# The first layer's transposed activations: by TensorE, or by a round trip through DRAM and 32x32 squares on VectorE

## The chip, the cores and the metric

The kernel runs on one core of one Trainium2 chip. The metric is the device time of one execution in microseconds, as the median of several runs; before the change it is 1163.4 us, the median of three runs that lie between 1161.4 and 1163.57 us. Everything is in float32. The engines are named as the profile names them: PE is TensorE (PEld is its weight load), DVE is VectorE, ACT is ScalarE, POOL is GpSimd, SP is SyncE, which here only issues DMAs.

## The reference

Four sequences (B = 4) of N = 1024 tokens with D = 256 channels pass two layers. Only the first is touched by the change:

```python
xn = layernorm(x)                         # no weights
x = x + attention(xn) + ffn(xn)           # first layer
#   attention: q = xn Wq, k = xn Wk, v = xn Wv; causal softmax(q k^T / 16) v;
#              layernorm(out + v) * gamma + beta; then Wfc, bfc
#   ffn:       relu(xn W1 + b1) W2 + b2, 1024 hidden units
xn = layernorm(x)
x = x + gated_linear_attention(xn) + top2_of_8_experts(xn)   # second layer
```

The second layer has a gated attention in groups of 64 tokens, and eight experts with low-rank additions, of which each token takes two.

## The kernel before, in words

**Tiles.** 128 tokens lie on the 128 partitions. The first layer works in 16 units of 256 tokens (two token tiles); unit `u` is part `p = u % 4` of sequence `b = u // 4`. Scores of a unit reach back over all units of its sequence, so a unit with p = 3 has about four times the score work of one with p = 0.

**A unit's steps**, as functions of `block_kernel`:

- `first(u)`: mean and variance of 256 tokens, and `xn` (tokens on partitions), on DVE with a little ACT. `xn` has seven buffers, so it runs well ahead.
- `first_turn(u)` (line 423): four PE transposes of 128x128 (line 427) put `xn` with its channels on partitions into a PSUM bank; ACT copies the bank to `xnT` in SBUF (line 429; six buffers). A matmul needs `xnT` wherever the contraction runs over channels.
- `queries(u)` (line 439): eight PE records on `xnT`, copied by ACT to `qT` (line 446).
- `scores(u, qT)` (line 449): `sc` in PSUM from `qT` and the `xnT` of all units of the sequence so far; DVE adds the mask (line 461) and takes the maximum (line 463), ACT the exponential (line 466), DVE the reciprocal and the scaling (lines 468, 469).
- `turns` (line 487): PE transposes of the attention weights; ACT copies those of the first token tile, DVE those of the second (line 495), to `attT`.
- `hidden` (line 473): the first matmul of the feed-forward part, `relu` on ACT (line 483).
- `weighted` (line 497): `pz` from `xn` and `attT`; DVE adds `xnT` and writes `zT` (line 507).
- `finish` (line 512): second feed-forward matmul `po` (line 520) and the value product `pv` (line 524), added to x by DVE (lines 526, 533).
- `norms`, `norms_turn`, `logits` (lines 537 to 587): norms for the second layer, four PE transposes (line 566), ACT copy to `xlT` (line 571) and, for b > 0, a store of `xlT` to DRAM (line 573).
- `merge` (line 379): loads a piece of an expert's weights (`wt`, `lt`), multiplies its low-rank pair on PE (lines 397 to 400), adds it on DVE (line 403) and stores the sum to DRAM (lines 404, 406). `fold_second` (line 349) does a small preparation once; its tile `bb` shares the buffers of `zT`.

**Order.** The loop at line 662 runs over the units. In iteration u stand: `turns(u)` and the first half of `hidden(u)`, `first_turn(u + 2)`, `queries(u + 1)`, `norms_turn(u - 1)`, `weighted(u)`, `logits(u - 1)`, `scores(u + 1)`, the rest of `hidden(u)`, `first(u + 3)`, `finish(u)`, `norms(u)`. The tile framework puts each engine's instructions into one fixed order when the program is built, by its own estimate of when each can start; on the chip every engine, and every engine's DMA queue, takes them strictly in that order and stands still at one that has to wait. PSUM banks of the first layer are four in rotation for nearly everything (`p_mm`, through `bank`), and two double banks for scores and `merge` (`p_sc`).

**After the first layer** come the second layer's attention for sequence 0, the table of experts, 36 blocks of 256 gathered tokens for the experts (`blocks`), and the attention of sequences 1 to 3 with the gathering and adding of the experts' results. The experts' blocks already use the way that the change brings to the first layer: `rows(i)` (line 792) reads 256 rows of 256 floats from DRAM with four DMAs of 64 KB that place runs of 32 floats so that each 32x32 square lies on its target partitions, and `turn` (line 810) transposes the squares with one DVE instruction (line 812).

Of the kernel before, what the change touches and what calls it, by code (L numbers as in the profile page):

```python
# [9 lines left out]
F32 = mybir.dt.float32  # L10
# [7 lines left out]
P = 128  # L18
B, N, D = 4, 1024, 256
NT = N // P  # L20
DC = D // P
# [41 lines left out]
def block_kernel(ctx: ExitStack, tc: tile.TileContext, x, wq, wk, wv, wfc, w1, w2, wqk, wvl, wg,  # L63
                 wo, wr, ew, el, eb2, cols, rows, rope, posb, out):
    nc = tc.nc
    pers = ctx.enter_context(tc.tile_pool(name="pers", bufs=1))
    small = ctx.enter_context(tc.tile_pool(name="small", bufs=3))
    NP = NT // 2
# [27 lines left out]
    def col(name, i=0):  # L96
        n = COLS[name][0] + i
        return colt[:, n : n + 1]

    def row(name):  # L100
        n, w = ROWS[name]
        return rowt[:, n - RE : n - RE + w]
# [56 lines left out]
    dram = ctx.enter_context(tc.tile_pool(name="dram", bufs=1, space=DRAM))  # L159
    wm13 = dram.tile([E, P, W13], F32, name="wm13")  # L160
    wm2 = dram.tile([E, P, W2B], F32, name="wm2")
    xg = dram.tile([E * RS, D], F32, name="xg")
    yg = dram.tile([NBLK * TB, D], F32, name="yg")
    xld = [dram.tile([P, DC, N], F32, name=f"xld{b}") for b in range(B)]

    def stats(src, mv, t, tag="st"):
        st = small.tile([P, 6], F32, tag=tag, name="st")
        w = nc.vector.bn_stats(st, src)  # L168
        nc.vector.bn_aggr(mv[:, t, :], st)  # L169
        return w.ins  # L170
# [21 lines left out]
    def rstd_of(var, tag, n=NT):  # L192
        rstd = small.tile([P, n], F32, tag=tag, name="rstd")
        rsqrt(rstd, var)
        return rstd

    def normalise(dst, src, mv, rstd, t):
        nc.vector.tensor_scalar(dst, src, mv[:, t, 0:1], rstd[:, t : t + 1], ALU.subtract, ALU.mult)
# [25 lines left out]
    with ExitStack() as l0:  # L224
# [7 lines left out]
        def bank(shape, name):  # L232
            return p_mm.tile(shape, F32, tag="mm", name=name)

        act = l0.enter_context(tc.tile_pool(name="l0a", bufs=2))
# [110 lines left out]
            return raw  # L346

        def fold_second(raw):
            bb = act.tile([P, DC, P], F32, tag="zT", name="bb")
            for c in range(DC):  # L350
                nc.gpsimd.tensor_copy(bb[:, c, :], col("ln1_b", c).to_broadcast([P, P]))
            for w, name, n in ((raw, "bqk", QK), (wvl_s, "bv", H1)):
                pm = bank([P, n], "pm")
                for c in range(DC):
                    nc.tensor.matmul(pm, bb[:, c, :], w[:, c, :], start=(c == 0), stop=(c == DC - 1))
                nc.vector.tensor_tensor(row(name), pm, row(name), ALU.add)
            pm = bank([P, HC], "pm")
            for m in range(HC):
                for c in range(DC):
                    nc.tensor.matmul(pm[:, m : m + 1], wg_s[:, c, ts(m, P)], col("ln1_b", c),  # L360
                                     start=(c == 0), stop=(c == DC - 1))
            n = COLS["bg"][0]
            nc.vector.tensor_tensor(bg_s, pm, colt[:, n : n + HC], ALU.add)
            with tc.issue_after(finish.sq):
                for c in range(DC):
                    nc.scalar.mul(wqr_s[:, c, 0:QK], raw[:, c, :], col("ln1_w", c))
                    nc.scalar.mul(wvl_s[:, c, :], wvl_s[:, c, :], col("ln1_w", c))
                    nc.scalar.mul(wg_s[:, c, :], wg_s[:, c, :], col("ln1_w", c))
            for dst, name in ((hg_s, "gamma"), (hb_s, "beta")):
                src = row(name).rearrange("p (i d) -> p i d", i=4)  # L370
                nc.gpsimd.tensor_copy(dst[:, 1], src)
                for i in range(4):
                    nc.gpsimd.tensor_copy(dst[:, 0, i], src[:, i ^ 1])
            for k in range(2):
                nc.gpsimd.tensor_tensor(fold[:, k, :], ident[:, 0:QK], ident[:, QK:P], ALU.add)
            nc.gpsimd.tensor_scalar(fold, fold, 1.0 / N, None, ALU.mult)
# [29 lines left out]
                nc.sync.dma_start(out=wm2[e, :, ts(c, HID)], in_=wt[:, 2, :])  # L406
            return multiply

        xns, xnTs = {}, {}


        def first(u):
            b, p = divmod(u, NP)
            xb = xs[b]
            mv = small.tile([P, 2, 2], F32, tag="mv0", name="mv")
            for i in range(2):
                first.stats = stats(xb[:, 2 * p + i, :], mv, i, "st0")
            rstd = rstd_of(mv[:, :, 1], "rstd0", 2)
            xn = xns[u] = act.tile([P, 2, D], F32, tag="xn", name="xn", bufs=7)
            for i in range(2):  # L420
                normalise(xn[:, i, :], xb[:, 2 * p + i, :], mv, rstd, i)

        def first_turn(u):
            pt = bank([P, DC, 2 * P], "pt")
            for i in range(2):
                for c in range(DC):
                    nc.tensor.transpose(pt[:, c, ts(i, P)], xns[u][:, i, ts(c, P)], ident)
            xnT = xnTs[u] = act.tile([P, DC, 2 * P], F32, tag="xnT", name="xnT", bufs=6)
            first_turn.copy = nc.scalar.copy(xnT, pt).ins
# [9 lines left out]
        def queries(u):  # L439
            pm = bank([P, DC, 2 * P], "pm")  # L440
            for m in range(DC):
                for c in range(DC):
                    nc.tensor.matmul(pm[:, m, :], qk_s[:, c, ts(m, P)], xnTs[u][:, c, :],
                                     start=(c == 0), stop=(c == DC - 1))
            qT = act.tile([P, DC, 2 * P], F32, tag="qT", name="qT")
            qTs[u] = nc.scalar.copy(qT, pm).ins  # L446
            return qT

# [48 lines left out]
        def weighted(u, attT):  # L497
            b, p = divmod(u, NP)
            pz = bank([P, DC, 2 * P], "pz")
            last = 2 * p + 1  # L500
            for c in range(DC):
                for j in range(last + 1):
                    q0 = P if j == last else 0
                    nc.tensor.matmul(pz[:, c, q0:], xns[b * NP + j // 2][:, j % 2, ts(c, P)],  # L504
                                     attT[:, j, q0:], start=(j == 0), stop=(j == last))
            zT = act.tile([P, DC, 2 * P], F32, tag="zT", name="zT")
            nc.vector.tensor_tensor(zT, pz, xnTs[u], ALU.add)
            return zT

# [51 lines left out]
        def norms_turn(u, xl):  # L561
            b, p = divmod(u, NP)
            pt = bank([P, DC, 2 * P], "pt")
            for i in range(2):
                for c in range(DC):
                    nc.tensor.transpose(pt[:, c, ts(i, P)], xl[:, i, ts(c, P)], ident)
            if b == 0:
                xlT = xl0[:, :, ts(p, 2 * P)]
            else:
                xlT = act.tile([P, DC, 2 * P], F32, tag="xlT", name="xlT")  # L570
            nc.scalar.copy(xlT, pt)
            if b:
                nc.sync.dma_start(out=xld[b][:, :, ts(p, 2 * P)], in_=xlT)
            return xlT
# [75 lines left out]

        U = B * NP
        first(0)
        fuse_scores()
        first_turn(0)
        with tc.issue_after(fuse_scores.qk), tc.issue_after(first_turn.copy):
            first(1)
        qT = queries(0)
        first_turn(1)
        ready = scores(0, qT)
        with tc.issue_after(scores.last):  # L660
            first(2)
        for u in range(U):
            b, p = divmod(u, NP)
# [6 lines left out]
            if u == 1:  # L670
                fold_second(raw)
# [10 lines left out]
            if u + 2 < U:  # L682
                first_turn(u + 2)
# [3 lines left out]
            if u + 1 < U:  # L687
                qT = queries(u + 1)
            if u:
                xlT = norms_turn(u - 1, xl)  # L690
            zT = weighted(u, attT)
            if u:
                logits(u - 1, xlT, lgs)
# [24 lines left out]
            if p == 0 and b:  # L718
                routed = route(b - 1, lgs)
            lgs = lg  # L720
        logits(u, norms_turn(u, xl), lgs)
        q = NT - 2
        send(b, *route(b, lgs, q, 2), q, 2)
# [500 lines left out]
```

## Time and profile before

| | us |
|---|---|
| median of three runs | 1163.4 |
| lowest and highest | 1161.4, 1163.57 |
| the profiled execution's own time | 1163.01 |
| its span, first to last instruction | 1161.3 |
| PE busy | 1142.0 |
| DVE busy | 547.1 |
| ACT busy | 303.7 |
| POOL busy | 176.0 |

The profile is one execution, recorded by the hardware. Its own time is 1163.01 us: 1161.3 us of span and 1.7 us around it. The granted PE clock is 0.999 over the span. Busy shares are averages over stages; the first layer is the first 530 us or so, the experts lie at about 580 to 936 us, and the second layer's attention of sequences 1 to 3 after them. A group of instructions in the profile gives the line of the kernel, engine, operation, result and sources, shapes and count, then the busy time; "idle before" says how long the engine stood still just before, and an arrow names what it was released by.

### The profile page before, as it was taken

The page shows a single profiled execution, that of the slowest core. Times are in us where ns is not written, and L with a number is a line of the kernel's source. Part 1 is how long each engine was busy: PE and PEld are TensorE (multiplying, and loading weights), DVE is VectorE, ACT ScalarE, POOL GpSimd, SP SyncE. Part 2 cuts the span into 40 slices and gives each one's busy share as a digit, 9 for nine tenths or more (in the row PEclk, how much of TensorE's full clock was granted, in tenths as well). Part 3 has the DMA queues.
Part 4 walks back from the last instruction along what each step waited for, and adds up shares of the span by engine and source line. Part 5 has one row for each costly group of instructions (what it writes and reads, how often), then busy time and mean ns, then how long its engine had stood idle before and what let it go on. Part 6 is the DMA issues. An engine that isn't in the chain of part 4 may idle for free. (4 is left out here: it accounts for less than half of the span.)

```text
span 1161.3 us, 15320 instructions
## 1 busy us (share of the span) xinstructions
PE 1142.0 (98%) x5308; PEld 896.7 (77%) x5308; DVE 547.1 (47%) x1486; ACT 303.7 (26%) x779; POOL 176.0 (15%) x209
## 2 busy tenths in 40 slices
PE   8999999999999999999999999999999999999997
PEld 6778878888878887874688888888888885554645
DVE  6442544345433344447663272232323324677855
ACT  3432333334323333225011121111111112122121
POOL 3200201123021213141000000000000003353410
PEclk9999999999999999999999999999999999999999
DMA  8510212232232232131658776677776642332211
GB/s 309 134 60 28 91 60 83 82 113 92 68 96 63 71 103 84 64 114 36 226 129 226 234 229 208 202 216 226 229 210 200 203 167 65 100 90 81 80 39 37
DMA packets 137552, 149.52 MB, mean 129 GB/s; under 512 B 84736, under 2 KB 109184, under 8 KB 132352
## 3 DMA queue, kind: packets, MB, share of 16 engines
q1 hardware_dynamic: 45360, 112.57, 29.0%
q10 hardware_dynamic: 85968, 19.15, 7.8%
q0 software_dynamic: 6144, 16.79, 4.6%
q8 instruction: 43, 0.70, 0.2%
q14 instruction: 37, 0.30, 0.1%
HBM read 107.84 MB, written 41.71 MB: 129 GB/s over the span
## 5 line engine op out<-in xcount | busy, mean ns | idle before, releaser
L824 PE MATMUL p<-xT,w 128*128 128x256 f32 x1152 | 254.6, 379 | 0.0
L824 PEld LDWEIGHTS p<-xT,w 128*128 128x128 f32 x1152 | 218.6, 190 | 30.3 <-issue 0.4
L829 ACT ACTIVATE s<-p,w 128x256 f32<-128x256 f32 x144 | 60.5, 471 | 332.3 <-PE p L824 317.6
L832 DVE SCALAR_TENSOR_TENSOR g<-p,w,s 128x256 f32<-128x256 f32 x144 | 62.9, 479 | 173.9 <-PE p L824 173.9
L883 POOL DMA_INDIRECT y<-yg,slot x64 | 65.1, 1017 | 510.5 <-PEq L868 429.4
L841 PE MATMUL py<-w,g 128*128 128x256 f32 x576 | 130.0, 379 | 0.0
L841 PEld LDWEIGHTS py<-w,g 128*128 128x128 f32 x576 | 109.4, 190 | 14.9
L480 PE MATMUL pm<-xnT,w_s 128*128 128x256 f32 x512 | 118.5, 379 | 0.0
L520 PE MATMUL po<-w_s,hT 128*128 128x256 f32 x512 | 116.1, 380 | 0.0
L520 PEld LDWEIGHTS po<-w_s,hT 128*128 128x128 f32 x512 | 96.8, 190 | 20.2 <-issue 8.0
L480 PEld LDWEIGHTS pm<-xnT,w_s 128*128 128x128 f32 x512 | 95.0, 190 | 11.6
L644 POOL DMA_INDIRECT xg<-xr,put x64 | 62.5, 976 | 167.2 <-ACT hT L483 75.7
L459 PE MATMUL sc<-xnT,qT 128*128 128x256 f32 (+1 forms) x320 | 65.8, 361 | 0.0
L504 PE MATMUL pz<-attT,xn 128*128 128x256 f32 (+1 forms) x320 | 65.0, 358 | 0.0
L504 PEld LDWEIGHTS pz<-attT,xn 128*128 128x128 f32 x320 | 57.1, 190 | 6.7
L958 PE MATMUL pv<-wvl_s,xl 128*128 128x512 f32 x128 | 57.6, 597 | 4.0 <-DVE v L960 3.9
L524 PE MATMUL pv<-vo_s,zT 128*128 128x512 f32 x128 | 60.2, 592 | 0.0
L459 PEld LDWEIGHTS sc<-xnT,qT 128*128 128x128 f32 x320 | 54.6, 191 | 6.0 <-ACT qT L446 0.2
L1076 PE MATMUL pj<-wo_s,gd 128*128 128x256 f32 x256 | 57.0, 381 | 1.1 <-DVE o L1078 0.6
L1029 PE MATMUL pg<-xl,wg_s 128*128 128x512 f32 x128 | 57.5, 593 | 0.0
L483 ACT ACTIVATE hT<-pm,colt 128x256 f32<-128x256 f32 x128 | 52.6, 466 | 13.9 <-PE pm L480 13.6
L843 DVE TENSOR_TENSOR yt<-py,w 128x512 f32<-128x512 f32 x36 | 24.9, 691 | 64.8 <-PE py L841 64.8
(226 smaller groups left out, 1315.3 us busy)
## 6 DMA issues: line engine op xcount, KB each, us to landing
w<-wm SPq DMA_DIRECT2D x36, 1028.0 KB
w<-wm SPq DMA_DIRECT2D x36, 640.0 KB
wt<-in_ew_dram SPq DMA_DIRECT2D x16, 768.0 KB
xt<-xg ACTq DMA_DIRECT2D x144, 64.0 KB
yg<-yt ACTq DMA_DIRECT2D x36, 256.0 KB
wm<-wt SPq DMA_DIRECT2D x16, 512.0 KB
wm<-wt SPq DMA_DIRECT2D x16, 256.0 KB
out_dram<-x SPq DMA_DIRECT2D x15, 256.0 KB
```

The costliest lines, as they stand in the source:

```text
L459: nc.tensor.matmul(sc[:, kp * 2 * P : kp * 2 * P + w], qT[:, c, ts(i, P)], xnTs[b * NP + kp][:, c, 0:w], start=(c == 0), stop=(c == DC - 1))
L480: nc.tensor.matmul(pm[:, j, :], w1_s[:, c, ts(2 * m2 + j, P)], xnTs[u][:, c, :], start=(c == 0), stop=(c == DC - 1))
L504: nc.tensor.matmul(pz[:, c, q0:], xns[b * NP + j // 2][:, j % 2, ts(c, P)], attT[:, j, q0:], start=(j == 0), stop=(j == last))
L520: nc.tensor.matmul(po[:, i, :], hT[:, m, ts(i, P)], w2_s[:, m, :], start=(m == 0), stop=(m == IC - 1))
L524: nc.tensor.matmul(pv, zT[:, c, ts(i, P)], vo_s[:, c, :, :], start=(c == 0), stop=(c == DC - 1))
L644: w = nc.gpsimd.indirect_dma_start(out=xg, out_offset=bass.IndirectOffsetOnAxis(ap=put[:, b * NT + t : b * NT + t + 1], axis=0), in_=xrs[b ...
L824: nc.tensor.matmul(p[:, j, :], w13[:, w0 : w0 + P], xT[:, c, :], start=(c == 0), stop=(c == DC - 1))
L829: nc.scalar.activation(s[:, j, :], p1[:, j, :], AF.Silu, bias=w13[:, EB1 + m : EB1 + m + 1])
L832: nc.vector.scalar_tensor_tensor(g[:, m, :], p3[:, j, :], w13[:, EB3 + m : EB3 + m + 1], s[:, j, :], ALU.add, ALU.mult)
L841: nc.tensor.matmul(py[:, k, :], g[:, m, ts(k, P)], w2[:, m * D : (m + 1) * D], start=(m == 0), stop=(m == EC - 1))
L883: w = nc.gpsimd.indirect_dma_start(out=ys[b][:, t, k, :], out_offset=None, in_=yg, in_offset=bass.IndirectOffsetOnAxis(ap=slot[:, n : n + ...
L958: nc.tensor.matmul(pv, a.xl[:, c, ts(t, P)], wvl_s[:, c, :], start=(c == 0), stop=(c == DC - 1))
```

## The change

For units 3 to 15 `first` now also calls a new function `strip`: SP stores `xn` to a DRAM tile `xnd`, and four SP DMAs read it back into a tile `strip` (two buffers), 32 floats at a run, so that each 32x32 square lies on its target partitions. `first_turn` of such a unit is one DVE instruction that transposes the squares from `strip` into `xnT`; the four PE transposes, the PSUM bank and the ACT copy of that unit are gone. Units 0 to 2 stay as they were. Four tiles that had two buffers have one: `bb`, `qT`, `zT` and `xlT`.

```diff
+    xnd = dram.tile([B * NP, 2 * P, D], F32, name="xnd")
...
-            bb = act.tile([P, DC, P], F32, tag="zT", name="bb")
+            bb = act.tile([P, DC, P], F32, tag="zT", name="bb", bufs=1)
...
-        xns, xnTs = {}, {}
+        xns, xnTs, strips = {}, {}, {}
...
+        def strip(u, rows):
+            nc.sync.dma_start(out=xnd[u].rearrange("(i p) d -> p i d", p=P), in_=rows)
+            w = strips[u] = act.tile([P, DC, 2 * P], F32, tag="strip", name="strip", bufs=2)
+            src = xnd[u].rearrange("(i r) (c j a) -> j r c i a", r=32, c=DC, a=32)
+            for j in range(4):
+                nc.sync.dma_start(out=w[32 * j : 32 * j + 32].rearrange("r c (i a) -> r c i a", a=32), in_=src[j])
...
         def first(u):
...
+            if u > 2:
+                strip(u, xn)
...
         def first_turn(u):
+            if u in strips:
+                xnT = xnTs[u] = act.tile([P, DC, 2 * P], F32, tag="xnT", name="xnT", bufs=6)
+                nc.vector.transpose(xnT, strips[u])
+                return
             pt = bank([P, DC, 2 * P], "pt")
...
-            qT = act.tile([P, DC, 2 * P], F32, tag="qT", name="qT")
+            qT = act.tile([P, DC, 2 * P], F32, tag="qT", name="qT", bufs=1)
...
-            zT = act.tile([P, DC, 2 * P], F32, tag="zT", name="zT")
+            zT = act.tile([P, DC, 2 * P], F32, tag="zT", name="zT", bufs=1)
...
-                xlT = act.tile([P, DC, 2 * P], F32, tag="xlT", name="xlT")
+                xlT = act.tile([P, DC, 2 * P], F32, tag="xlT", name="xlT", bufs=1)
```

## The prediction

> **What bounds the kernel now.** I read the page's busy rows first, then the busy times by window for the stretch that the change touches, then PE's own waits there, and last the instructions of the turned tiles one by one. The chain of waits is no help: it covers only the end, from 965 us on, and the first layer isn't in it.
>
> ```profile
> PE 1142.0 (98%) x5308; PEld 896.7 (77%) x5308; DVE 547.1 (47%) x1486; ACT 303.7 (26%) x779; POOL 176.0 (15%) x209
> ...
> 48.00:545.00 497.00, 494.15 (x2404) 395.74 (x2403) 222.06 (x725) 175.19 (x501) 94.43 (x89) 1.00 0.23 78
> ...
> PE pt L427 <- DVE attT L495: 1.1, 3, 0.4
> PE prk L625 <- DVE both L615: 1.1, 1, 1.1
> PE pm L443 <- DVE attT L495: 0.4, 1, 0.4
> PE pt L566 <- DVE xl L551: 0.2, 1, 0.2
> ```
>
> The second line is the stretch of units 1 to 15: length, then busy PE, PEld, DVE, ACT, POOL, the granted clock, DMA share (0.23) and GB/s. PE works 494.15 of 497.00 us at full clock; DVE has over half of its time free, ACT two thirds. The last four lines are all that PE waits for another engine there: 2.8 us. So the stretch is as long as PE's list of work, and what leaves that list shortens the run unless a new wait appears.
>
> **Removed from PE and ACT.** The merged PE timeline shows what four transposes take of PE, from their start to the next group's (start, length, instruction; lengths overlap, starts count):
>
> ```profile
> 178.74 0.60 PE L427 MATMUL pt<-ident,xn 128*128 128x128 f32 x4
> 179.18 1.89 PE L443 MATMUL pm<-xnT,qk_s 128*128 128x256 f32 x8
> ...
> 151.45 0.60 PE L427 MATMUL pt<-ident,xn 128*128 128x128 f32 x4
> 151.99 1.99 PE L443 MATMUL pm<-xnT,qk_s 128*128 128x256 f32 x8
> ...
> 86.17 0.66 PE L427 MATMUL pt<-ident,xn 128*128 128x128 f32 x4 [0.36 <-DVE attT L495]
> 86.67 1.89 PE L443 MATMUL pm<-xnT,qk_s 128*128 128x256 f32 x8
> ```
>
> The thirteen distances are 0.43, 0.50, 0.49, 0.54, 0.44, 0.50, 0.49, 0.55, 0.44, 0.49, 0.49, 0.54 and 0.43: together 6.33 us. The 0.36 us ahead of the third I don't count: it waits for DVE's attT copy to free a PSUM bank, and with one bank less in the rotation `queries` inherits that wait. The 13 ACT copies (7.59 us) were never waited for by PE; they count nothing.
>
> [...]
>
> **Added to DVE.** The experts' `turn` is the same instruction on the same shape:
>
> ```profile
> L812 DVE STREAM_TRANSPOSE xT<-xt x36: 696/702/712, 583.6 to 934.9; 128x512 f32<-128x512 f32 x36
> ...
> L797 ACTq DMA_DIRECT2D xt<-xg x144: 588/605/2533, 578.6 to 909.2; - x144
> ...
> 578.57 5.42 ACTq L797 DMA_DIRECT2D xt<-xg  x7
> 583.60 0.71 DVE L812 STREAM_TRANSPOSE xT<-xt 128x512 f32<-128x512 f32 x1 [0.79 <-DMA xt<-xg]
> ```
>
> 13 x 0.70 = 9.1 us on DVE, put where the built order of the changed program puts them. By the times of before, eleven fall into holes in which DVE waits for something else: unit 3 at 50.7 (hole 1.2 us), 4 at 64.6 (1.1), 5 at 69.6 (3.4), 6 at 99.2 (1.2), 7 at 140.2 (2.4), 9 at 163.5 (3.1), 10 at 223.8 (1.2), 11 at 264.9 (2.3), 13 at 288.1 (3.2), 14 at 348.4 (1.2), 15 at 384.0 (5.0). These cost nothing; the cover is the waiting for ACT's exponential or rs, or for PE's po. Units 8 and 12 have no hole: they stand in `norms` between lines 543 and 544 and push `xl` from 152.6 to about 153.1, while `norms_turn`, now 0.54 earlier, wants it at 153.3. Bounds 0 to 0.5 each; I take 0.1, as the estimate leaves 0.2 us of room.
>
> **Added to SP, and the new waits.** Per unit a 256 KB store (the nearest row, the store of xlT, takes SP 0.59 us) and four loads (0.605 each): 3 us of issue, 39 in all. SP stands waiting most of the layer, so nothing behind is late by more than a few us: `wt` and `lt` come some 25 us ahead of their `merge`. A transpose is ready when the store has landed and four loads have followed. From the first load's issue to the use the row above shows 5.0 us (578.57 to 583.60, DVE waiting). No row gives the store's landing in DRAM: I bound it by 1.5 us (the loads above start to move data that long after issue) and 4 us (from issue of the stores at 48.67 to past the end of their traffic at 52), and take 3, nearer the stores. So 8 us after `xn` when the DMA engines are free.
>
> Two places are close. Unit 7: `xn` is done at 129.0, but x and wt issued at 124.3 and 124.8 keep the engines full to 131.1; store landed at 133, strip at 138, the DVE slot is at 140.2, and DVE's holes up to 147.7 would hide a start as late as 145.5. Units 11 and 15 are alike or easier. Unit 3: the store queues behind `wt` near 39, lands at about 46, loads are issued to 48.5 and land behind the second `wt` at 50 to 51.5. Behind this transpose on DVE stand the attT copy and `xl`, which PE wants at 56.3; they need 2.4 us, so a start up to 53.9 costs nothing. Bounds 0 and 3; I take 0.3. The other units' strips are back long before their slot.
>
> **One buffer.** `qT`, `zT` and `xlT` of unit u + 1 are written after PE has read unit u's by PE's own order, and the store of `xlT` is issued within 1 us, some 27 us before the next. Cost 0. `bb` must now wait until `finish(0)` has read `zT`: PE's last pv ends at about 45.3, POOL's two copies need 0.66 (before: at 34.27), ready at 46.0; PE wants the second half at about 46.4; behind `bb` POOL has nothing to do before 53.0. Bounds 0 and 0.5; I take 0.
>
> **Sum.** -6.33 + 0.2 (units 8, 12) + 0.3 (unit 3) = -5.8 us. Against the profiled execution's own 1163.01 us (span 1161.3 and 1.7 around it) that is 1157.2; it stands 0.4 below the median of 1163.4, from which the sum would be 1157.6. I put 1157.4. Behind the layer everything shifts: PE works 49.33 of the 50 us from 530 to 580 and all of 620 to 936, so the gain isn't caught by a later wait.
>
> **The rivals.** [...]
>
> *DVE hands the time back.* PE runs 0.49 us earlier per unit, DVE works 0.70 more. If each transpose delayed the next attT copy or `xl` by half of its length, 13 x 0.35 = 4.5 us come back: 1161.8; with a quarter 1159.6. For it: the PE waits above are all on DVE. Against: the holes listed.
>
> *The place doesn't bind.* If the experts' start hung on POOL's scatter or the table, the gain would vanish: 1163. Only PE's 0.7 us of idle from 530 to 580 speaks for it.
>
> **How the numbers follow.** A measurement of this kernel can tell about 0.2%, 2.3 us, from no change. Forecast 0.74, its own range 1156.0 to 1159.5; time handed back 0.12, about half of it still faster by over 2.3 us; not binding 0.03; late strips 0.11. Faster 0.80, same 0.09, slower 0.11. The range runs from 1155.5 (all of 6.33, and some of the waits on banks gone) to 1162.5, which takes in most of the handed-back case.
>
> **What would show it.** Right: PE busy lower by 6 to 8 us, idle in the stretch still near 3 us, 49 transposes, not 36, of 0.70 us on DVE, none of them with a wait for a DMA over 1 us but unit 3's. Wrong: DVE waiting for strip for several us with PE's attT or xl waits behind it; SP's `wt` loads late; or PE's idle time up by as much as its work went down.

## The result and the profile after

| | before | after |
|---|---|---|
| median, same chip, in turn | 1162.21 us | 1159.15 us |
| ratio (95% interval) | | 0.9971 (0.9959 to 0.9982) |
| a second comparison | 1164.8 us | 1161.7 us |
| its ratio | | 0.9968 (0.9957 to 0.998) |
| profiled execution: own time, span | 1163.01, 1161.3 us | 1158.1, 1155.3 us |

The changed kernel is faster by 3.1 us, both times by the medians. The forecast was 5.8: its direction and its range (1155.5 to 1162.5) held, but the interval of the first ratio (2.1 to 4.8 us of gain) doesn't reach 5.8. Nearly half of the gain is missing, and the rest of this text looks for it. The two profiled spans differ by 6.0 us; that is no evidence for the forecast, as will be seen.

The lines that answer to those shown of before are the page's busy row, the stretch from 48 to 545 us (length, then busy PE, PEld, DVE, ACT, POOL, granted clock, DMA share, GB/s), and what PE waited for in that stretch (us, times, longest). `first_turn`'s lines are gone, so later lines have moved: `queries` is L460, `norms_turn` L583, the copy of `xlT` L588, `logits` L600, DVE's `xl` L568.

```profile
PE 1137.0 (98%) x5256; PEld 891.9 (77%) x5256; DVE 554.6 (48%) x1499; ACT 297.2 (26%) x766; POOL 176.0 (15%) x209
...
48.00:545.00 497.00, 493.53 (x2363) 392.94 (x2362) 234.57 (x745) 172.15 (x492) 94.20 (x89) 1.00 0.29 91
...
PE pm L460 <- DVE attT L512: 1.4, 4, 0.4
...
PE pl L600 <- ACT xlT L588: 0.3, 1, 0.3
PE pl L600 <- ACT xl L588: 0.3, 1, 0.3
PE pt L583 <- DVE xl L568: 0.2, 1, 0.2
```

PE lost 52 instructions and 5.0 us of work, DVE took 7.5 us more, ACT gave up 6.5. The wait for `attT` (0.36 us, four times) now stands wholly at `queries`: three of the four stood at the removed transposes, as forecast. New are two waits of `logits` for ACT. So nothing large went wrong. The added work itself shows in two rows: VectorE's turns, and the loads of the strips with the time from issue to landing.

```profile
L439 DVE STREAM_TRANSPOSE xnT<-strip x13: 695/703/711, 51.0 to 381.3; 128x512 f32<-128x512 f32 x13
its engine sat idle before it (us, times) until:
  DMA strip<-xnd: 0.9, 1
...
L420 SPq DMA_DIRECT2D strip<-xnd x52: 557/630/2027, 45.5 to 378.8; - x52
...
DMA to landing us min/median/max: 2.3/2.8/6.2
```

One of 13 turns waited for its strip, 0.9 us (unit 15's), and PE felt nothing of it. In this trace the way through DRAM is hidden.

To see where time went inside the layer I set the start of `queries` of each unit in the two traces side by side. For units 2 to 15, after minus before:

| unit | 2 | 3 | 4 | 5 | 6 | 7 | 8 | 9 | 10 | 11 | 12 | 13 | 14 | 15 |
|---|---|---|---|---|---|---|---|---|---|---|---|---|---|---|
| us | -0.11 | -0.61 | -1.00 | -1.44 | -1.46 | -1.96 | -2.34 | -2.79 | -2.80 | -3.30 | -3.69 | -4.13 | -4.54 | -4.55 |

Where a step was meant to bring 0.43 to 0.55, three kinds of places brought less. Unit 2 has -0.11 instead of -0.43: PE's first `pv` of `finish(0)` came 0.31 late, before any new instruction had run; in the changed kernel's second profile this 0.3 is absent, so it was chance. From unit 5 to 6 and from 9 to 10 almost nothing came (-0.02, -0.01 instead of -0.44). And behind units 3, 4, 7, 8, 11 and 12 there is 0.1 less each, and behind unit 15 another 0.2 is lost. (No turn was removed in the step from 14 to 15.)

All later comparisons use one length that start-up and tail don't touch: from `queries` of unit 2 to the first matmul of the experts' table. I call it the layer; its last 31 us also hold the first products of the second layer. It is read so, before above, after below:

```profile
55.00 1.89 PE L443 MATMUL pm<-xnT,qk_s 128*128 128x256 f32 x8
...
550.10 0.28 PE L738 MATMUL pn<-seen,ones 128*128 128x8 f32 x2
```

```profile
54.89 1.89 PE L460 MATMUL pm<-xnT,qk_s 128*128 128x256 f32 x8
...
545.74 0.28 PE L755 MATMUL pn<-seen,ones 128*128 128x8 f32 x2
```

495.10 us became 490.85, so 4.25 us. Twelve of the thirteen removals lie inside it, 6.33 - 0.43 = 5.90 us by the forecast's distances. So 1.65 us is lost in this stretch, and more outside it.

The larger loss inside is the step from unit 5 to 6, where the forecast had found no hole for the turn of unit 8. First DVE's order there before the change, then all engines after it:

```profile
150.43 0.15 DVE L543 TENSOR_TENSOR var<-mean,rstd 128x2 f32<-128x2 f32 x1
150.61 0.16 DVE L544 TENSOR_TENSOR var<-var,rstd 128x2 f32<-128x2 f32 x1
151.37 0.16 DVE L546 TENSOR_TENSOR rstd<-rstd 128x2 f32<-128x2 f32 x1 [0.60 <-ACT rstd L175]
...
151.85 0.73 DVE L551 TENSOR_SCALAR xl<-x,mean,rstd 128x256 f32<-128x256 f32 x2
```

```profile
149.53 0.15 DVE L560 TENSOR_TENSOR var<-mean,rstd 128x2 f32<-128x2 f32 x1
149.60 0.70 DVE L439 STREAM_TRANSPOSE xnT<-strip 128x512 f32<-128x512 f32 x1
150.23 0.12 DVE L561 TENSOR_TENSOR var<-var,rstd 128x2 f32<-128x2 f32 x1
...
150.38 0.30 ACT L175 ACTIVATE rstd<-var,epst 128x2 f32<-128x2 f32 x1 [0.99 <-DVE var L561]
150.55 1.89 PE L460 MATMUL pm<-xnT,qk_s 128*128 128x256 f32 x8
...
151.36 0.73 DVE L568 TENSOR_SCALAR xl<-x,mean,rstd 128x256 f32<-128x256 f32 x2
151.81 0.91 ACT L572 ACTIVATE xr<-xl,inv 128x256 f32<-128x256 f32 x2 [0.68 <-DVE xl L568]
...
153.33 0.58 ACT L463 COPY qT<-pm 128x512 f32<-128x512 f32 x1
153.80 0.60 ACT L588 COPY xl<-pt 128x512 f32<-128x512 f32 x1
...
154.45 1.11 PE L600 MATMUL pl<-wqr_s,xl 128*128 128x72 f32 x8 [0.26 <-ACT xl L588]
```

Measured from the start of `queries`, `xl` began 0.14 us before it in the kernel before and 0.81 after it now. PE's transposes of `xl` (L583) still came through without a wait. But ACT runs `xr`, two `relu`, the copy of `qT` and the copy of `xlT` in this order, each behind the other, and the last of them now ends after PE wants it for `logits`. The price is 0.42 us here and 0.43 for unit 12. That is a reading of one trace so far; the experiments test it.

### The profile page after: what moved, and what is told of

The parts are those of the page before. It is cut to its first block, busy times and chain, and to the rows that moved or that the text cites. A ratio compares the mean times of both kernels' runs of the same rounds, so it can differ in the third digit from the quotient of the medians.

```text
span 1155.3 us, 15325 instructions
## 1 busy us (share of the span) xinstructions
PE 1137.0 (98%) x5256; PEld 891.9 (77%) x5256; DVE 554.6 (48%) x1499; ACT 297.2 (26%) x766; POOL 176.0 (15%) x209
```

## The experiments

In each table the layer is the length defined above. Ratios are to the kernel before, on the same chip.

**First: where the gain is lost.** Four kernels. The first moves the two turns:

```diff
-                nc.vector.transpose(xnT, strips[u])
+                with tc.issue_after(norms.last[u - 5]) if u in (8, 12) else nullcontext():
+                    nc.vector.transpose(xnT, strips[u])
...
-            nc.vector.tensor_scalar(xl[:, i, :], ...)
+            norms.last[u] = nc.vector.tensor_scalar(xl[:, i, :], ...).ins
```

> The changed kernel, but VectorE takes the turns of units 8 and 12 only after the `xl` of the step in which they stand. Theory (the gain misses about 1 us because those two turns hold up `xl`, then ScalarE's copy of `xlT` that the logits wait for, 0.4 to 0.5 us each): both steps give the loss back, the first layer's end moves from 545.74 to about 544.9, and the time is 0.8 to 1.0 us under the changed kernel's, some 4 us (0.35%) under the kernel before. Rival (VectorE's added 9 us cost time wherever they stand): another step loses the same 0.5 us and the layer's end stays within 0.2 us of 545.74. Rival (0.36 us waits on `attT` at `queries` are the whole loss): no change either.

The second is the kernel before with `bufs=1` for `bb`, `qT`, `zT` and `xlT`:

> The kernel before, with only the one-buffer part of the change (bb, qT, zT, xlT). Theory: it costs nothing; the first layer's end within 0.3 us of the 550.10 of before and the time within 0.1% of it. Rival (what the gain lacks was lost by waits for these buffers): 1.3 to 2.5 us longer than before, with waits of TensorE or of the copies ahead of lines that write the four tiles.

The third adds without removing:

```diff
-                xnT = xnTs[u] = act.tile([P, DC, 2 * P], F32, tag="xnT", name="xnT", bufs=6)
-                nc.vector.transpose(xnT, strips[u])
-                return
+                spare = act.tile([P, DC, 2 * P], F32, tag="spare", name="spare", bufs=1)
+                nc.vector.transpose(spare, strips[u])
```

> The changed kernel with all 52 TensorE transposes and 13 ScalarE copies kept; the strips go through DRAM and are turned by VectorE as well, into a spare tile that nobody reads. So it has what the change adds without what it takes away. Theory: the added work costs about 1 us (0.5 in each of the two steps where a turn stands ahead of `xl`, nothing elsewhere), layer's end at about 551, time 0.05 to 0.15% over the kernel before. Rival (VectorE hands its time back in most steps, 13 x 0.2 to 0.35 us): 2.6 to 4.5 us over it, 0.22 to 0.4%. Rival (the transfers disturb the stream of the experts or the end of the kernel): a later end with the layer's end unchanged.

The fourth leaves the way through DRAM out (`strips[u] = xn` in place of `strip(u, xn)`):

> The changed kernel without the way through DRAM: VectorE turns the squares of `xn` where they stand, which leaves out the exchange of squares between the four groups of 32 partitions, so the queries see other numbers; stores and loads (13 and 52 transfers) are gone, and the turns follow their `xn` at once. Theory (the way through DRAM is hidden): within 1 us of the changed kernel, the difference being where the turns fall between VectorE's other lines; units 3 to 5 now turn at 25 to 31 us. Rival (the transfers and their landing cost the missing part of the gain): 1.5 to 3 us under the changed kernel, spread over the steps.

| | layer, us | ratio (95% interval) |
|---|---|---|
| before | 495.10 | |
| after | 490.85 | 0.9971 (0.9959 to 0.9982) |
| turns of 8 and 12 behind `xl` | 490.00 | 0.9976 (0.9969 to 0.9983) |
| one buffer only | 495.06 | 1.0003 (0.9996 to 1.0009) |
| added work only | 495.82 | 1.0024 (1.0016 to 1.0033) |
| no DRAM | 489.81 | 1.0326 (1.0312 to 1.034) |

Inside the layer the theory held in all four. Moving two instructions brought 0.85 us, and the trace shows them out of the way, `xl` ahead of the turn and `logits` without a wait:

```profile
152.97 1.89 PE L461 MATMUL pm<-xnT,qk_s 128*128 128x256 f32 x8
...
153.38 0.72 DVE L569 TENSOR_SCALAR xl<-x,mean,rstd 128x256 f32<-128x256 f32 x2
...
154.02 0.70 DVE L440 STREAM_TRANSPOSE xnT<-strip 128x512 f32<-128x512 f32 x1
...
156.46 0.78 PE L601 MATMUL pl<-wqr_s,xl 128*128 128x72 f32 x5
```

The buffers cost nothing. The added work costs 0.72 us, and without DRAM the layer is only 0.2 shorter than with it and `xl` first. So 13 round trips through DRAM cost at most 0.2 us in the layer, and probably nothing: the 0.2 lies behind unit 15 alone, and a run below with 14 round trips doesn't have it.

The times tell another story. With the turns moved, the layer is 5.1 us shorter than before, the time only 2.8 (2.0 to 3.6). The added work lengthens the layer by 0.7 and the time by 2.8 (1.9 to 3.8). In both, some 2 us go outside the layer. The time of the fourth kernel says nothing: my expectation overlooked that other queries give other routes. Its experts do 1248 matmuls of `p` instead of 1152 (39 blocks, not 36), and PE stands 8.4 us once; only its layer can be compared.

**Second: what happens outside the layer.** The added work again without its transfers; the changed kernel again; the changed kernel with strips that come later; and unit 2 turned by DVE as well, on top of the moved turns. The first leaves out the way through DRAM as above, with all results kept, since the spare tile isn't read:

```diff
-                strip(u, xn)
+                strips[u] = xn
```

The second has no edit. The third is this, with the strips then read from `xnd2`:

```diff
+            if u > 3:
+                nc.sync.dma_start(out=xnd2[u], in_=xnd[u])
```

And the fourth:

```diff
-            if u > 2:
+            if u > 1:
                 strip(u, xn)
```

> As the run with the added work only (all TensorE transposes kept, VectorE's turns go to a spare tile), but the turns take `xn` where it stands: the 13 stores and 52 loads are gone, every result stays the same. It asks why that run was 2.6 us over the kernel before when its first layer lost only 0.7. Theory (the transfers through DRAM cost some 1.5 us outside the first layer: in the time around the span, which was 2.1 us there against 1.7 before, and in waits for the experts' weights): at most 0.6 us (0.05%) over the kernel before, 1.7 us around the span, fewer waits for `w`. Rival (VectorE's turns or the changed layout of memory do it): 2 to 3 us over it, as with the transfers.

> The changed kernel once more, on one chip with the others. Theory: first layer's end, from the queries of unit 2 on, as in its first profile (490.85 us, 4.25 less than before); the time 2.5 to 3.3 us under the kernel before, the rest lost in waits for the experts' weights (0.3 to 1 us) and around the span (0.1 to 1 us). Rival (the missing part was chance of one profile and one chip): 4 us or more under it.

> The changed kernel with a second copy within DRAM between store and loads for units 4 to 15, so that their strips come 3 to 4 us later. Theory (there is room behind VectorE's slots): units 7, 11 and 15 make VectorE wait 1 to 4 us, which PE doesn't feel; layer from the queries of unit 2 on 490.9 to 491.4 us; and if transfers cost time around the span, more of it (over 2.2 us). Rival (a late strip is paid in full): 3 us at each of the three units, layer at 497 to 500, some 8 us longer. Rival (half the places): one of the three is paid, 2 to 3 us.

> The version with VectorE's turns of units 8 and 12 behind `xl`, and unit 2 taken through DRAM as well (14 units instead of 13). Theory: another 0.4 to 0.5 us of TensorE's list is gone, stretch to the layer's end from the queries of unit 2 on as in the first of these runs (490.0) with those queries 0.4 earlier, time 0.3 to 0.5 us under that run, 4 us under the kernel before at best. Rival (unit 2's strip is late, since its store queues behind the loads of x and the weights at 30 to 45 us): VectorE waits for it with the copies of `attT` behind, and the start is 1 to 4 us later.

| | layer, us | ratio (95% interval) |
|---|---|---|
| added work without DRAM | 495.15 | 1.0003 (0.9994 to 1.0011) |
| after, again | 490.85 | 0.9968 (0.9957 to 0.998) |
| two trips | 490.14 | 0.9955 (0.9942 to 0.9969) |
| unit 2 too | 489.81 | 1.0024 (1.0016 to 1.0031) |

Without transfers the added turns cost nothing that the time shows (0.3 us, -0.7 to 1.3), though in the profile 1.7 us are lost ahead of the layer, between `queries` of units 1 and 2, where VectorE's first turns now stand in the start-up. So the loss outside comes with the transfers. But it isn't their number: two trips have 12 more and are no slower (the intervals overlap), and their time around the span is 1.74 us, as before (1.72), not over 2.2. That part of my theory fell.

Two trips missed my expectation for the layer as well, in the other direction (490.9 to 491.4). DVE waited for a strip once, 1.0 us (unit 13's), and PE felt none of it. The gain of 0.7 over the changed kernel comes from where the turns of units 8 and 12 now lie. Unit 12's is behind `xl`, as in the run that moved it; its step is 0.3 shorter. Unit 8's, whose step is 0.4 shorter, lies here:

```profile
150.93 0.16 DVE L564 TENSOR_TENSOR var<-var,rstd 128x2 f32<-128x2 f32 x1
151.11 0.71 DVE L442 STREAM_TRANSPOSE xnT<-strip 128x512 f32<-128x512 f32 x1
151.75 0.12 DVE L566 TENSOR_TENSOR rstd<-rstd 128x2 f32<-128x2 f32 x1
```

It stands one instruction later, behind the second `var`. There DVE used to wait 0.60 us for ACT's square root (the 0.60 in the rows of before), and the 0.7 us fill that hole. One place earlier, the same instruction delays the square root itself. With later strips the framework chose better places.

With unit 2 the rival had the direction, but not the way: DVE turned the strip at 36.89 us without a wait for it. The loss is larger than the rival's 1 to 4, 8.3 us ahead of the stretch measured: from `queries` of unit 1 to those of unit 2 it takes 37.97 us instead of 29.69. It comes through SP's queue. There the strip's loads wait for the store of `xn` to land (SP did so five times in the changed kernel, 5.4 us at most), and the loads behind them wait too. Start, length and DMA, first in the changed kernel, then with unit 2:

```profile
28.79 6.84 SPq L323 DMA_DIRECT2D wm<-in_eb_dram  x8
36.41 1.42 SPq L385 DMA_DIRECT2D lt<-in_el_dram  x3
```

```profile
26.51 3.12 SPq L420 DMA_DIRECT2D strip<-xnd  x4
...
35.23 6.02 SPq L323 DMA_DIRECT2D wm<-in_eb_dram  x8
42.89 2.31 SPq L385 DMA_DIRECT2D lt<-in_el_dram  x3
```

`lt`, which `merge` wants at 45.6 us, is issued 6.5 us later. From `merge` to the next `turns` PE takes 10.2 us instead of 5.0, and meanwhile its clock falls: 0.89 over 50 to 52 us, 0.50 to 60, 0.55 over 60 to 62, then 1.00 again. Two rows of it, at half and at full clock (PE, PEld, DVE, ACT and POOL busy, the granted clock third from the end):

```profile
52.00:54.00 2.00, 2.00 (x4) 0.84 (x4) 1.90 (x6) 0.58 (x2) 0.00 (x0) 0.50 0.69 207
...
62.00:64.00 2.00, 2.00 (x12) 1.77 (x11) 1.31 (x2) 0.50 (x3) 0.00 (x0) 1.00 0.00 0
```

PE counts as busy in both, so only the clock column tells the difference. Some 10 us at half speed are about 5 of the 8.3 us lost (an estimate from these rows). The rest I put down to the late loads; no run separates the two.

**Third: the queue's place.** Comparing SP's issues in the experts' stage, I found a difference that goes with the loss. Between two issues of `w` (19 us after the experts' start) SP takes 0.58 or 0.59 us in the kernel before, with one buffer only, with the added work without DRAM, with two trips and with unit 2 too; in the changed kernel (twice), with the turns moved and with the added work through DRAM it takes 0.94 or 0.95. These four profiles are those with exactly 65 transfers added on SP. The load then arrives 0.36 us later and PE waits for it. To test it, five stores of 256 bytes are added on SP, which do nothing but move its later instructions by five places:

```diff
+            if 10 <= u <= 14:
+                nc.sync.dma_start(out=pad[u : u + 1, :], in_=rows[0:1, 0, 0:64])
```

> The version with VectorE's turns of units 8 and 12 behind `xl`, and five stores of 256 bytes more on SP's queue (one row of `xn` of units 10 to 14 into a spare tensor), which only move the later instructions of that queue by five places. Theory (in the changed kernel SP takes 0.9 us instead of 0.58 between two issues of `w` loads, 19.2 instead of 18.9 us after the experts' start, in every run with 13 units through DRAM once, in none with 5 or 12 transfers more: a matter of where the instructions lie; TensorE waits 0.3 to 0.7 us for that load): gap 0.58, no wait for `w` in the second pair of groups (31 us after the experts' start at most 31.0, against 31.0 + 0.3 to 0.7), layer as before (490.0 us from the queries of unit 2 on), time 0.3 to 0.8 us under the run without the five stores. Rival (chance, or the traffic of the strips): the gap stays 0.9 and the wait comes.

The next one tries for the 0.1 us steps as well:

```diff
-                copy = nc.vector.tensor_copy if i else nc.scalar.copy
+                copy = nc.vector.tensor_copy if i and (t < 4 or j0) else nc.scalar.copy
```

> As the run with SP shifted, and the first copy of `attT` of the odd tile goes to ScalarE in steps 2 and 3 of each batch (8 copies), so that the bank that `queries` needs is no longer freed by VectorE behind `xl`. Theory (what removal of the transposes didn't bring in these steps is the wait of 0.36 us and its restart of 0.1 that `queries` inherited): 4 x 0.46 = 1.8 us less, layer from the queries of unit 2 on 487.9 to 488.5, best of all versions, 5 to 6.5 us under the kernel before. Rival (ScalarE's copies push `relu` of hidden or the copy of `qT` back): 0 or a loss of up to 8 x 0.4 = 3 us.

> The version with the turns of units 8 and 12 behind `xl` once more, on one chip with the two others. Theory: layer 490.0 us from the queries of unit 2 on, 0.9 us gap on SP and a wait for `w` 27.7 to 28.5 us after the experts' start as in its first run; 3 to 4.5 us under the kernel before, 0.3 to 0.8 us over the shifted one. Rival (the shift does nothing): both the same.

> The changed kernel itself with only the five small stores on SP's queue (units 8 and 12 turned ahead of `xl`, as it does). Theory (the place of SP's instructions is an own part of what the change cost, beside the 0.84 us of the two late `xl`): gap between the `w` issues 0.58 instead of 0.9, no wait for `w` 27.7 to 28.5 us after the experts' start, layer unchanged at 490.85 us from the queries of unit 2 on; time 0.5 to 1.2 us less than the changed kernel's -3.1 and -3.7 of its two comparisons, so 3.6 to 4.9 us under the kernel before, and some 0.8 over the version with both edits (-5.6). Rival (the 5.6 us of that version were chance or came from `xl` alone): 3.1 to 3.4 us under it, as without the stores.

| | turns moved | SP shifted | layer, us | `w` issues apart, us | ratio (95% interval) |
|---|---|---|---|---|---|
| after, again | no | no | 490.85 | 0.95 | 0.9968 (0.9957 to 0.998) |
| after, shifted | no | yes | 490.95 | 0.59 | 0.9962 (0.9949 to 0.9976) |
| turns moved, again | yes | no | 490.03 | 0.94 | 0.9964 (0.9952 to 0.9976) |
| turns moved, shifted | yes | yes | 490.05 | 0.59 | 0.995 (0.9937 to 0.9963) |
| the last with copies on ACT | yes | yes | 490.38 | 0.59 | 0.9963 (0.9951 to 0.9975) |

The shift did to the gap and the wait what the theory said. With the turns moved, first SP's issues and PE's timeline without the shift, then the same with it:

```profile
601.70 0.33 SPq L826 DMA_DIRECT2D w<-wm  x1
602.64 0.33 SPq L824 DMA_DIRECT2D w<-wm  x1
...
611.77 2.61 PE L843 MATMUL p<-xT,w 128*128 128x256 f32 x11 [0.46 <-DMA w<-wm]
```

```profile
602.36 0.34 SPq L829 DMA_DIRECT2D w<-wm  x1
602.95 0.33 SPq L827 DMA_DIRECT2D w<-wm  x1
...
611.80 2.54 PE L846 MATMUL p<-xT,w 128*128 128x256 f32 x11
```

The gap and the wait are gone together, in all three profiles with the shift. By the medians the shift is worth 1.3 us here (1157.6 to 1156.26, on one chip), more than the 0.3 to 0.8 expected; the intervals of the two ratios still overlap, and PE's delay there is 0.29 to 0.69 us in the five profiles that have it. So it is shown that moving the queue's later instructions by five places takes the wait away; that the wait makes all of the 1.3 us is not. What SP does in the 0.36 us no record here tells.

The end of the kernel changes with the shift too. DVE's last instruction, without the shift (span 1155.8 us) and with it (1155.5):

```profile
1152.12 0.48 DVE L1108 SCALAR_TENSOR_TENSOR x<-o,rstdo,x 128x256 f32<-128x256 f32 x1
```

```profile
1152.21 0.48 DVE L1111 SCALAR_TENSOR_TENSOR x<-o,rstdo,x 128x256 f32<-128x256 f32 x1
```

From its end to the end of the span it is 3.2 and 2.8 us. All profiles with 65 added transfers have 3.1 to 3.2 there, as has the one with unit 2, which has no gap; those without transfers have 2.7 to 2.8, those with the shift or two trips 2.8 to 3.0. In these two profiles the wait for `w` (0.65), this tail (0.4) and the time around the span (0.1, by the medians) make 1.1 of the 1.3 us.

The changed kernel with the shift alone is 4.2 us faster than before by the medians, as expected, but within what two comparisons of it can differ by.

Copies on ACT failed: the four waits for DVE are gone, and in the p = 3 steps others take their place.

```profile
PE pm L464 <- ACT hT L504: 1.2, 3, 0.4
```

Steps with p = 2 gained 0.26 us, those with p = 3 lost 0.38, and the layer is 0.3 longer than without the edit.

The version with both edits, turns moved and SP shifted, is the best measured: 5.6 us under the kernel before, ratio 0.995, against 3.1 us for the change as it was made.

## Why the prediction was right, and where its sum was off

*PE bounds the stretch, so what leaves its list shortens the run.* Right. Its waits for other engines in the stretch stayed small, 3.3 us against 2.8. But PE's work fell by 5.0 us, where I had named 6 to 8 as the sign.

*6.33 us removed.* Right. The steps with nothing in their way brought 0.50, 0.50 and 0.50 us in the changed kernel (ahead of the queries of units 3, 7 and 11), against distances of 0.50, 0.50 and 0.49; the run agrees with the trace.

*`queries` inherits the wait for `attT`, at no cost.* Half right. The wait moved as said. But in both traces a `queries` group whose weight load starts behind a wait takes 1.83 or 1.84 us to the next group, where the others take 1.72 or 1.73, and so loses 0.1 us. `queries` of unit 3 after the change, to be compared with 86.67 and 88.40 before:

```profile
86.06 1.99 PE L460 MATMUL pm<-xnT,qk_s 128*128 128x256 f32 x8 [0.36 <-DVE attT L512]
87.90 0.60 PE L583 MATMUL pt<-ident,xl 128*128 128x128 f32 x4
```

In the kernel before, the removed transposes had this start in their distance; now `queries` has it, in units 3, 7 and 11 and also in 4, 8 and 12. Six times 0.1 make 0.6 us that my sum did not have. The 0.2 behind unit 15 are something else: there DVE comes 0.2 us later to a sum of `merge`, and two groups on PE behind it, the second half of `hidden` and the transposes of `xl`, start 0.1 later each. Nothing in the trace says why.

*Units 8 and 12: 0.1 each.* The step that failed. I compared the new `xl` with the nearest reader, `norms_turn`, and saw 0.2 us of room there. That held, it has no new wait, and the sizes were right: from the first `var` of the rows above to `xl` it is 0.41 us longer (0.5 forecast) and to `queries` 0.54 shorter (0.54 forecast). But the tight reader was two engines on, ACT's chain from `xr` to the copy of `xlT` and `logits` behind it, and I hadn't followed it. Measured: 0.42 and 0.43, together 0.85 as the moved turns showed. With the 0.8 above, this is all of the 1.65 us lost in the stretch; the 0.85 is shown by experiment, twice, the 0.8 is read from the traces.

*Unit 3: 0.3; other strips in time; one buffer 0; `bb` 0.* Right but for the 0.3, which was 0: the turn started at 50.99, where the limit was 53.9. Two trips showed that the others have room: unit 7 was turned at 143.27 instead of 140.79 (the changed kernel's second profile), at no cost. The one strip that was waited for was unit 15's (0.9 and 1.23 us in the two profiles), which I had called as easy as unit 7's or easier. The forecast kept 0.11 for late strips, but no run shows a way through DRAM that is slow enough for it: in the changed kernel a 64 KB load of a strip landed in 2.8 us (median). Late strips are out for the change as made. With unit 2 too it was not the strip that came late, but what stood behind its loads on SP's queue.

*DVE hands its time back.* Out as a rule for every step: in most nothing, in two 0.42 us.

*Behind the layer everything shifts.* The other step that failed. 4.7 us arrive at the layer's end by the changed kernel's second profile (from `queries` of unit 1: 520.10 instead of 524.79 us), and 3.1 in the time. I took the later stages as given, but 65 more transfers on SP's queue moved its later instructions, and one load of `w` became late by 0.36 us. That costs PE 0.3 to 0.7 us, the tail is 0.4 us longer, and the time around the span grew by 0.1 in the second comparison (1.80 instead of 1.72 us by the medians; in the first, four of the seven runs had 2.7 to 3.2). In the second profile the three make 1.1 of the 1.6 us. The other 0.5 stays open and is within what a comparison of seven runs can miss. A second wait for `w`, near 860 us, is no part of it: it comes and goes (0.37 us in that profile, none in that of before, 0.25 with one buffer only, 0.63 with both edits). Why 65 transfers act so stays open too.

The near agreement of the two profiled spans with the forecast (6.0 us) was luck: 2.0 us of it lie at the end, where PE waits for `v` in the second layer, 3.9 us in four waits before and 1.9 in two after. Other profiles have 1.9 or 3.1 to 3.8, with the change (3.1 in its second) and without it. That the measured 1159.15 us lies in the forecast's own range (1156.0 to 1159.5) owes something to luck too: the median of before was 1162.21 us in that comparison, 1.2 under the 1163.4 that the forecast set out from.

## What to carry to other kernels

When an instruction is added to an engine with much free time, follow what it delays through every queue behind it to the first reader that waits, not only to the next one; and place it in a gap in which that engine waits anyway, since one place earlier or later decided 0.4 us here. Compare stretches between two marks in the trace rather than whole spans, which start-up (0.9 to 2.7 us here) and the end (2.0 us) move too. Look at the DMA queue as well: with unit 2 too, loads that waited for a store to land held up what is issued behind them by 6.4 and 6.5 us, and added transfers shift the place of later instructions on that queue. Here that went with a load late by 0.36 us and a tail longer by 0.4, and five tiny transfers more took most of it away.

## What the runs showed of the hardware

**Half clock in the start-up.** In eight of the fourteen profiles PE's granted clock fell to 0.50 between 21 and 28 us, for 3 to 7 us; in six it stayed at 1.00. Two stretches of the first run with the turns moved, which had the fall, and then the same two of the changed kernel's first profile, which had not (columns as above, the clock third from the end):

```profile
18.00:22.00 4.00, 2.16 (x13) 1.32 (x11) 3.17 (x13) 2.33 (x8) 0.00 (x0) 0.91 1.11 370
22.00:26.00 4.00, 3.44 (x9) 2.61 (x9) 3.23 (x12) 1.34 (x4) 1.39 (x6) 0.50 1.02 411
```

```profile
18.00:22.00 4.00, 2.16 (x14) 1.30 (x12) 3.49 (x14) 2.12 (x7) 0.00 (x0) 1.00 1.11 371
22.00:26.00 4.00, 3.41 (x17) 2.96 (x17) 4.00 (x16) 1.54 (x6) 1.52 (x6) 1.00 1.00 406
```

In both PE is busy for 2.16 us of 18 to 22. `queries` of unit 1 start at 25.3 to 25.8 us without the fall and at 26.7 to 28.1 with it. The moved turns had it in one profile and not in the other. What sets it off no run shows. Small shifts of the start-up go with it: `queries` of unit 0 started 10.97 to 11.12 us into the span in the eight profiles with the fall, and 11.20 to 11.70 in the six without; of 18 to 20 us PE was busy for 0.57 to 0.71 us in the eight, and for 0.80 to 1.30 in the six. Between two profiles of this kernel such a fall goes with 0.9 to 2.7 us.

**VectorE beside GpSimd.** While POOL ran seven additions of 128x512 (27.04 to 36.02 us in the changed kernel), DVE's two `xn` took 1.68 us. At 22.94 us the same two instructions took 0.72.

```profile
26.88 1.68 DVE L199 TENSOR_SCALAR xn<-x,mv,rstd 128x256 f32<-128x256 f32 x2
27.04 8.98 POOL L452 TENSOR_TENSOR x<-x,bias 128x512 f32<-128x512 f32 x7
```

The scaling of `att` takes longer too: 1.33 us for 128x384 within these 9 us, 0.49 for 128x512 right after them. Not every DVE instruction does: `zT` took 0.68 us there (0.67 to 0.69 elsewhere). The profile of before has the same pattern (`xn` 1.69 us beside POOL, 0.72 at 22.40). No run here takes POOL's additions away, so whether the two engines disturb each other is not shown.
